# Moving and tying steps in a four-layer graph network kernel on Trainium2: normalisation, root rows, score vectors, diagonal and feature sums

## The chip, the core and the metric

The kernel runs on one core of one Trainium2 chip. The metric is device time in microseconds (us) of one execution. Work is spread over five engines, each with its own queue that it works through in order: TensorE (PE in the profile; its weight loads are PEld), VectorE (DVE), ScalarE (ACT), GpSimd (POOL) and SyncE (SP), which here only issues transfers. An engine that needs what another makes waits at that instruction, and everything behind it in its queue waits too.

## The reference

The input is `x` (2708 x 512, fp32), a sparse but densely stored adjacency `adj` (2708 x 2708) and the weights. Four layers, each followed by a residual and a layer normalisation:

```python
deg = max((adj != 0).sum(-1), 1)
# layer 0: the positive mask, divided by the root of its row count, is added to adj
head = mask / max(sqrt((mask * mask).sum(-1)), EPS)          # mask = adj > 0
inc = adj + head
x = layernorm(x + (inc @ x) / inc.sum(-1))
# layer 1: gated sum of an attention and a plain graph convolution
gate_a = sigmoid(concat(adj @ x, x) @ Wa.T + ba)              # gate_b alike with Wb, bb
h = x @ W_sa
s_left, s_right = h @ a_sa[:D], h @ a_sa[D:]
e = where(adj != 0, exp(-leaky_relu(s_left[:, None] + s_right[None, :])), 0)
x_a = (e / (e.sum(1) + 1e-5)) @ h
x_b = adj @ (x @ W_gcn) + b_gcn
x = layernorm(x + sigmoid(gate_a * x_a + gate_b * x_b))
# layer 2: three hops
p = x; out = x @ w[0]
for i in 1..3: p = adj @ p; out = out + p @ w[i]
x = layernorm(x + out)
# layer 3: degree-normalised convolution with self loops, and a skip
a_norm = rsqrt(deg)[:, None] * (adj + I) * rsqrt(deg)[None, :]
x = layernorm(x + relu((a_norm @ x + x) @ W + b))
```

## The kernel before

**Tiling.** The 2708 rows are two halves of 1354, each of 11 tiles of 128 rows (the last is partly filled). `KT` is 11, `HD` 256, `D` 512, `DC` 4. Each large product `adj @ X` in fp32 is a sweep: it works with the four quarters of the matrix (11, 12, 21, 22) and of the features (B11, B12, B21, B22) and forms seven products instead of eight, as in Strassen's scheme. For this VectorE makes sums of matrix tiles (`comb`, L403; in the later sweeps L1226) and sums of features, named T1 to T4 (`sums`, L352 to L355; L224 in the first sweeps). TensorE accumulates the products in PSUM banks (`accu`, `accc`, `accd`, `acca`), by L458 and L467 in sweeps 0 to 2 and by L1281 in sweeps 3 to 6. VectorE and ScalarE carry the results out. The letters A, B, C and D behind a name are groups of 3, 2, 3 and 2 of the ten full tiles, one SBUF buffer with room for three tiles each; the third part of a B or D buffer ("spare part") can hold other data.

**The sweeps.** Sweep 0 is layer 0, with the matrix prepared on the way: ScalarE turns raw tiles into masks (`mask`, L712 and L713), TensorE counts them (`cnt`, L724), VectorE takes the inverse root of the counts (`count_row`, L743 to L753, with one root on ScalarE, L749), TensorE spreads the roots over all partitions by transposes (`pr`, L761, in `spread_row`), ScalarE copies them out (`row`, L764), and VectorE adds mask times root to each matrix tile (`prep0`, L779 and L780). Each output tile is normalised in `done0`: statistics on VectorE (L555, L557, L559, L562), the power on POOL (`rstd`, L560), the scaling on ScalarE (L565), then the store to DRAM (`X<-o`, L149, POOL). Sweep 1 is `adj @ x` for layer 1. In it the score vectors are spread over the partitions, and each tile of x is multiplied with them (`score`, L923), which gives `s_left`, `s_right` and the gates' shares (`scores_end`, L928 and following); `score_rows` and, for the degrees, `rows` send them to DRAM as rows through `to_rows` (L937 transpose `ps_r`, L939 copy, L940 store). Sweep 2 is the attention, sweeps 3 to 5 the hops, sweep 6 layer 3, which adds the scaled diagonal to tiles of the matrix or of its saved sums (`As`) by `add_diag` (L1240).

**The score vectors before.** `start0` makes `vmat`: on each of 128 partitions, for each of four chunks of the features and each of four vectors, one value (L856, L859). `spread_v` transposes each chunk of each vector, broadcast over 128 columns, on TensorE (`pv`, L911, 16 transposes), and ScalarE copies the halves (L914, 8 copies) into eight spare parts of sweep 1's features.

**Order.** The kernel is a list of events, `at(position, function, hold)`. Positions are in units, 28 of them to a sweep (sweep s starts at 28 s; one of the seven products of a range of columns is about one unit). The list is sorted by position and run once to build the program; a tile framework then orders instructions by its own priorities and inserts the waits. `hold` ties an event's instructions behind the one before them on their engine in the list. So a shift of a position can also change the built order of other instructions.

```python
for p, _, fn in sorted(events, key=lambda e: e[:2]):
    fn()
...
    p = last if n < 3 * strict else done if n in held else {}
```

Of the kernel before, what the change touches and what calls it, by code (L numbers as in the profile page):

```python
# [68 lines left out]
def gnn_kernel(ctx: ExitStack, tc: tile.TileContext, x, adjT, w_sa, a_sa, w_gcn, b_gcn, wab, bab, w_hop, w_out,  # L69
# [48 lines left out]
    vmat = const.tile([P, DC, 4], F32, name="vmat")  # L118
# [4 lines left out]
    def feature(nm):  # L123
# [8 lines left out]
            for R0, w in RANGES for h in range(2)}  # L132
    DROW = [dram.tile([1, KT * P], F32, name=f"DR{h}", tag=f"DR{h}") for h in range(2)]
# [168 lines left out]
    def next_x2(base, src, ext_src=None, one=False, plus=False, swapped=False):  # L302
# [43 lines left out]
        def sums(g):  # L346
            i = slice(0, 2 if g in "BD" and ext_src is None else 3)
            part = lambda t: t[:, i, :]
            for s in ("T1", "T2", "T4"):
                group(s, g)  # L350
            t = {s: part(groups[s, g][0]) for s in SETS}
            nc.vector.tensor_tensor(t["T1"], t["T3"], t["B11"], ALU.subtract)  # L352
            nc.vector.tensor_tensor(t["T2"], t["B22"], t["T1"], ALU.subtract)
            nc.vector.tensor_tensor(t["T3"], t["B22"], t["T3"], ALU.subtract)
            nc.vector.tensor_tensor(t["T4"], t["B21"], t["T2"], ALU.subtract)  # L355
            for s in ("T1", "T2", "T3", "T4"):
                groups[s, g][1].update(range(3))
# [12 lines left out]
        for i, g in enumerate("ACBD"):  # L370
            at(base + 4.2 + 0.3 * i, lambda g=g: sums(g), True)


    def sweep(base, ranges, prep=None, extra=None, done=None, first=False, late=None, sums=False, save=False):
        A, spare = {}, {}
        nk = KW
        for r, (R0, n) in enumerate(ranges):
# [35 lines left out]
            if plain:  # L413
                when = {"11": (-4.0, 0.2), "12": (-3.8, 0.2), "21": (-2.4, 0.4), "22": (-1.6, 0.4)}
                pw = {"11": (-0.9, 0.6), "12": (-0.3, 0.6), "21": (3.3, 0.9), "22": (4.1, 0.9)}
# [137 lines left out]
    def layernorm(dsts, y, w, on_scalar=False):  # L553
# [9 lines left out]
        for d, c0, c1 in dsts:  # L563
            if on_scalar:
                nc.scalar.activation(d[:w], y[:w, c0:c1], AF.Identity, bias=rstd[:w, 0:1], scale=rstd[:w, 1:2])  # L565
                continue
# [228 lines left out]
    def extra0(pb, r, R0, n, A):  # L795
        if r == 0:
            for h, p, d in ((0, -3.7, 0.05), (1, 1.9, 0.055)):
# [12 lines left out]
                at(pb + p + d * 22 + 0.1 * h, lambda h=h: spread_row(R0, n, h))  # L810
        if r + 1 < len(RANGES0):
            R1, n1 = RANGES0[r + 1]
            for h, p, d in ((0, 1.0, 2.5), (1, 3.8, 2.5)) if r else ((0, 3.2, 2.2), (1, 5.4, 2.1)):
# [6 lines left out]
                at(pb + p + d + 0.15, lambda h=h: spread_row(R1, n1, h))  # L820
# [7 lines left out]
    def done0(p0, dp, last, R0, n, h, C, tiles):  # L828
        for i, (t, lo, w) in enumerate(tiles):
# [5 lines left out]
            def b(t=t, lo=lo, w=w, got=got):  # L835
# [3 lines left out]
                o = targets(t, last and not h, "o")  # L839
                layernorm(o, y, w, not last)  # L840
                store(X1[t], o, w)
# [3 lines left out]
            at(p, b)  # L845

    def start0():
# [4 lines left out]
        for n in range(2):  # L852
            v = nat("va")
            nc.scalar.dma_start(out=v, in_=bcast(a_sa[:, n * D : (n + 1) * D], D))
            for c in range(DC):
                nc.vector.scalar_tensor_tensor(y, ws[c], 1.0, v, ALU.mult, ALU.mult,  # L856
                                               accum_out=vmat[:, c, n : n + 1])
        for c in range(DC):
            nc.vector.tensor_copy(vmat[:, c, 2:4], wab_sb[:, DC + c, :])  # L859
            nc.vector.tensor_copy(wab_pad[:, c, 0:2], wab_sb[:, c, :])  # L860
# [44 lines left out]
    def spread_v():  # L905

        homes = [spare_part(s, g) for g in "BD" for s in ("B11", "B22", "T1", "T2", "T3", "B21")][:8]
        for j in range(4):
            ps = bank("pv")
            for c in range(DC):  # L910
                nc.tensor.transpose(ps[:, c * P : (c + 1) * P], vmat[:, c, j : j + 1].to_broadcast([P, P]), ident)  # L911
            for e in range(2):
                V[j, e] = homes[2 * j + e]
                nc.scalar.copy(V[j, e], ps[:, e * HD : (e + 1) * HD])  # L914

    at(S[1] + 0.85, spread_v)
# [38 lines left out]
    for R0, n in RANGES:  # L955
        for h in (1, 0):
            for k in tiles_of(R0, n):
# [3 lines left out]
                at(S[1] + 0.7 + 0.95 * i, go)  # L961
                at(S[1] + 1.1 + 0.95 * i, lambda t=h * KT + k, w=wt(k): score(t, w, got1))
                i += 1
            at(S[1] + 1.12 + 0.95 * (i - 1), lambda R0=R0, h=h, ts=tiles_of(R0, n): scores_end(R0, h, ts))
            at(S[1] + 1.6 + 0.95 * (i - 1), lambda R0=R0, h=h, ts=tiles_of(R0, n): score_rows(R0, h, ts))
    at(S[1] + 1.13 + 0.95 * (i - 1), scores_over)

    def extra1(pb, r, R0, n, A):
# [37 lines left out]
        at(pb + 3.2, lambda: rows(1))  # L1006
        at(pb + 5.2, lambda: end(0))
        at(pb + 5.8, lambda: rows(0))
# [186 lines left out]
    def sweep2(base, ext, done, on_diag=False):  # L1195
        nk = K2 + ext
        u = 2 / 7
        for g, (i0, n) in enumerate(RANGES2):
            Q, C = {}, {}
            for j, m in enumerate(ORDER2[g]):  # L1200
# [42 lines left out]
                for p, q, pos in ((0, 0, -0.52), (1, 0, -0.51), (1, 1, 0.59), (0, 1, 4.04)):  # L1243
                    for k in range(nk) if on_diag and op != "12" else ():
                        at(b + u * (pos + 0.8 * k / nk), lambda p=p, q=q, k=k, f=add_diag: f(p, q, k))
# [369 lines left out]
```

## Time and profile before

| what | value |
|---|---|
| median of 3 runs | 2874.45 us (2873.52 to 2877.68) |
| profiled execution | 2874.17 us |
| its span in the trace | 2872.1 us |
| mean granted TensorE clock | 0.998 |
| TensorE busy | 2826.4 us, 98% |
| VectorE busy | 2197.7 us, 77% |
| ScalarE busy | 546.3 us, 19% |
| GpSimd busy | 617.6 us, 22% |
| moved by DMA | 510.04 MB, mean 178 GB/s |

In a line of a group or of the timeline stand the start, the length, the engine, the line of the kernel, the instruction, the tile it writes and the tiles it reads, shapes, and the number of instructions taken together (x8); in brackets the idle time of the engine before it, and what ended it. A line of the waits reads: engine, its tile and line, what it waited for, the total in us, how often, the longest. A stretch of 361 us is one sweep.

### The profile page before, as it was taken

Reading aid. Unit: us, or ns where it says so; the run is one execution under the profiler, and the core shown is the slowest. Engines: PE = TensorE matmul, PEld = TensorE weight load, DVE = VectorE, ACT = ScalarE, POOL = GpSimd, SP = SyncE. Lnnn points to the kernel's source line nnn. Section 1 sums busy time; section 2 is a strip of 40 time slices with the busy share of each in tenths; the row PEclk is TensorE's granted clock in tenths of the full one; section 3 lists DMA queues with packets and bytes.
Section 4 is the critical chain, followed back from the end, with each engine's and each line's share of the span. In section 5 each row is a group of like instructions: output and inputs, shape, how many; then the busy total and the mean of one; then the engine's idle time right before and its main releaser. Section 6 shows DMA issues by size and latency. Waiting matters only on the chain. (4 is left out here: it accounts for less than half of the span.)

```text
span 2872.1 us, 37476 instructions
## 1 busy us (share of the span) xinstructions
PE 2826.4 (98%) x10963; PEld 1870.2 (65%) x10963; DVE 2197.7 (77%) x5670; ACT 546.3 (19%) x1119; POOL 617.6 (22%) x1113
## 2 busy tenths in 40 slices
PE   7999999999999999999999999999999999999998
PEld 5656665658765656766666666666666666666665
DVE  6989799667636554655699788887888878799987
ACT  4554200101146444641100000000000100100001
POOL 0223233223310101123213033030330211501202
PEclk9999999999999999999999999999999999999999
DMA  7666466355534333565668667566675665754542
GB/s 232 204 200 191 143 213 225 114 163 167 191 107 135 111 115 97 168 193 153 202 203 242 204 193 239 172 209 197 198 234 173 187 196 177 228 172 146 177 141 92
DMA packets 368524, 510.04 MB, mean 178 GB/s; under 512 B 63424, under 2 KB 321700, under 8 KB 368320
## 3 DMA queue, kind: packets, MB, share of 16 engines
q1 hardware_dynamic: 302392, 370.56, 43.8%
q0 software_dynamic: 49344, 126.38, 13.1%
q10 hardware_dynamic: 16584, 10.71, 1.3%
q8 instruction: 87, 1.43, 0.2%
q14 instruction: 117, 0.96, 0.1%
HBM read 423.77 MB, written 83.65 MB: 177 GB/s over the span
## 5 line engine op out<-in xcount | busy, mean ns | idle before, releaser
L1226 DVE TENSOR_TENSOR z<-z 128x339 f32<-128x339 f32 (+1 forms) x966 | 454.6, 504 | 12.6 <-PE accu L1281 3.4
L1299 ACT COPY q<-accu 128x338 f32<-128x338 f32 (+1 forms) x84 | 34.6, 443 | 1004.5 <-PE accu L1281 1002.7
L560 POOL TENSOR_TENSOR rstd<-rstd,neg_half 128x1 f32<-128x1 f32 (+3 forms) x91 | 59.3, 652 | 755.8 <-DVE rstd L559 494.9
L1281 PE MATMUL accc<-s,t 128*128 128x338 f32 (+1 forms) x644 | 198.2, 450 | 0.0
L1281 PE MATMUL accu<-z,t 128*128 128x338 f32 (+1 forms) x644 | 194.0, 448 | 1.5 <-DVE z L1226 1.5
L1281 PE MATMUL accd<-z,t 128*128 128x338 f32 (+1 forms) x644 | 193.9, 448 | 0.6 <-DVE q L1363 0.6
L1281 PE MATMUL accc<-z,t 128*128 128x338 f32 (+1 forms) x644 | 193.5, 448 | 0.5 <-ACT q L1299 0.5
L1414 POOL DMA_DIRECT2D Y<-y x192 | 105.0, 553 | 366.7 <-DVE y L1409 333.7
L403 DVE TENSOR_TENSOR a<-a,a 128x384 f32<-128x384 f32 (+2 forms) x330 | 162.6, 511 | 22.5 <-PE accu L458 21.7
L1281 PEld LDWEIGHTS accc<-s,t 128*128 128x128 f32 x644 | 120.9, 190 | 64.1 <-issue 7.5
L1281 PEld LDWEIGHTS accc<-z,t 128*128 128x128 f32 x644 | 122.0, 190 | 61.6 <-issue 1.0
L1281 PEld LDWEIGHTS accu<-z,t 128*128 128x128 f32 x644 | 121.7, 190 | 61.7 <-DVE z L1226 2.0
L1281 PEld LDWEIGHTS accd<-z,t 128*128 128x128 f32 x644 | 121.9, 190 | 60.5 <-DVE q L1363 1.5
L1226 DVE TENSOR_TENSOR s<-z 128x338 f32<-128x338 f32 (+1 forms) x322 | 149.7, 503 | 12.7 <-PE accc L1281 8.4
L1305 DVE TENSOR_TENSOR q<-q,accd 128x338 f32<-128x338 f32 (+1 forms) x112 | 56.0, 500 | 115.1 <-PE accd L1281 115.1
L1082 DVE SCALAR_TENSOR_TENSOR a<-a,e 128x384 f32<-128x384 f32 (+2 forms) x160 | 77.4, 507 | 51.0 <-ACT e L1081 46.3
L1080 ACT ACTIVATE e<-row,s_right 128x384 f32<-128x384 f32 (+5 forms) x176 | 96.5, 569 | 76.1 <-PE accc L458 20.4
L979 DVE SCALAR_TENSOR_TENSOR deg<-a,deg 128x384 f32<-128x384 f32 (+2 forms) x152 | 75.8, 505 | 13.6 <-DMA a<-in_adjT 11.9
L406 POOL DMA_DIRECT2D As<-a x120 | 64.9, 544 | 73.0 <-DVE a L403 70.2
L779 DVE SCALAR_TENSOR_TENSOR s<-a,row 128x384 f32<-128x384 f32 (+2 forms) x152 | 75.1, 507 | 6.0 <-ACT row L764 6.0
L1081 ACT ACTIVATE e<-e 128x384 f32<-128x384 f32 (+5 forms) x176 | 79.4, 477 | 1.8
L606 PE MATMUL ps_d<-w,xT 128*128 128x512 f32 (+1 forms) x176 | 79.2, 593 | 0.4 <-ACT xT L597 0.4
(683 smaller groups left out, 5840.4 us busy)
## 6 DMA issues: line engine op xcount, KB each, us to landing
z<-As SPq DMA_DIRECT2D x320, 169.5 KB
z<-As SPq DMA_DIRECT2D x320, 169.0 KB
a<-in_adjT SPq DMA_DIRECT2D x240, 192.0 KB
z<-in_adjT SPq DMA_DIRECT2D x240, 169.5 KB
z<-in_adjT SPq DMA_DIRECT2D x240, 169.0 KB
a<-in_adjT SPq DMA_DIRECT2D x120, 165.0 KB
a<-in_adjT SPq DMA_DIRECT2D x112, 128.0 KB
As<-a POOLq DMA_DIRECT2D x60, 192.0 KB, 3.9
```

What stands on the lines that cost most here:

```text
L403: nc.vector.tensor_tensor(A[r, dst, k][:, :n], A[r, a, k][:, :n], A[r, b, k][:, :n], op)
L406: nc.gpsimd.dma_start(out=SD[m][k * P : (k + 1) * P, R0 : R0 + n], in_=A[r, dst, k][:, :n])
L560: nc.gpsimd.tensor_tensor(rstd[:w, 1:2], rstd[:w, 0:1], neg_half[:w], ALU.pow)
L606: nc.tensor.matmul(o, lhs(c), r, start=c == 0 and n == 0, stop=c == DC - 1, skip_group_check=True)
L779: nc.vector.scalar_tensor_tensor(t[:w, :n], a[:w, :n], 0.0, row[R0, h][:w, :n], ALU.is_gt, ALU.mult)
L979: nc.vector.scalar_tensor_tensor(d[:w, :n], a[:w, :n], 0.0, d[:w, :n], ALU.not_equal, ALU.add)
L1080: nc.scalar.activation(e[:w, :n], row[R0, h][:w, :n], AF.Prelu, bias=s_right[:w, t : t + 1], alpha=0.01)
L1081: nc.scalar.activation(e[:w, :n], e[:w, :n], AF.Exp, scale=-1.0)
L1082: nc.vector.scalar_tensor_tensor(a[:w, :n], a[:w, :n], 0.0, e[:w, :n], ALU.not_equal, ALU.mult)
L1226: nc.vector.tensor_tensor(d[:, :n], Z[x + (k,)][:, :n], Z[y + (k,)][:, :n], op)
L1281: nc.tensor.matmul(B[home][:, :n], stat(v, k), a[:, :n], start=bool(start and k == 0), stop=k == nk - 1, skip_group_check=True)
L1414: nc.gpsimd.dma_start(out=rows[:, :, f * P : (f + 1) * P], in_=o[32 * f : 32 * (f + 1), : m * P].rearrange("p (b d) -> p b d", d=P))
```

## The change

Line numbers are those of the kernel before.

- Roots: `spread_row` of the first range is listed 0.18 instead of 0.1 units after `count_row` (half 1), and of later ranges 0.4 or 0.25 instead of 0.15.
- Normalisation: in `done0` the scaling L565 and the store leave event `b` and become events of their own 0.28 units later; the scaling is tied.
- Score vectors: `vmat` is laid out vector by vector; at position 10.3 one transpose, one copy and one transfer write it to DRAM (`VROW`, tag VR), and `spread_v` becomes eight broadcast transfers from there on SP's queue, at sweep 1's position 1.6 instead of 0.85.
- Scores: fetch, products and `scores_end` 1.2 units later, `score_rows` 1.9, degree rows 0.5.
- Feature sums: T1 and T2 stay at 4.2, T3 goes to 7.4 and T4 to 9.2, all tied.
- Diagonal: `add_diag` is tied for the first stage of the first group (`g == j == 0`).
- Preparation of quarters 21 and 22 in the first range: 0.1 units later.

```diff
@@
-    vmat = const.tile([P, DC, 4], F32, name="vmat")
+    vmat = const.tile([P, 4, DC], F32, name="vmat")
@@
+    VROW = dram.tile([4 * DC, P], F32, name="VR", tag="VR")
@@
-        def sums(g):
+        def sums(g, n):
             i = slice(0, 2 if g in "BD" and ext_src is None else 3)
             part = lambda t: t[:, i, :]
-            for s in ("T1", "T2", "T4"):
-                group(s, g)
+            if n == 0:
+                for s in ("T1", "T2", "T4"):
+                    group(s, g)
             t = {s: part(groups[s, g][0]) for s in SETS}
-            nc.vector.tensor_tensor(t["T1"], t["T3"], t["B11"], ALU.subtract)
-            nc.vector.tensor_tensor(t["T2"], t["B22"], t["T1"], ALU.subtract)
-            nc.vector.tensor_tensor(t["T3"], t["B22"], t["T3"], ALU.subtract)
-            nc.vector.tensor_tensor(t["T4"], t["B21"], t["T2"], ALU.subtract)
-            for s in ("T1", "T2", "T3", "T4"):
-                groups[s, g][1].update(range(3))
+            if n == 0:
+                nc.vector.tensor_tensor(t["T1"], t["T3"], t["B11"], ALU.subtract)
+                nc.vector.tensor_tensor(t["T2"], t["B22"], t["T1"], ALU.subtract)
+                for s in ("T1", "T2", "T3", "T4"):
+                    groups[s, g][1].update(range(3))
+            elif n == 1:
+                nc.vector.tensor_tensor(t["T3"], t["B22"], t["T3"], ALU.subtract)
+            else:
+                nc.vector.tensor_tensor(t["T4"], t["B21"], t["T2"], ALU.subtract)
@@
-            at(base + 4.2 + 0.3 * i, lambda g=g: sums(g), True)
+            for n, p in enumerate((4.2, 7.4, 9.2)):
+                at(base + p + 0.3 * i, lambda g=g, n=n: sums(g, n), True)
@@
-                pw = {"11": (-0.9, 0.6), "12": (-0.3, 0.6), "21": (3.3, 0.9), "22": (4.1, 0.9)}
+                pw = {"11": (-0.9, 0.6), "12": (-0.3, 0.6), "21": (3.4, 0.9), "22": (4.2, 0.9)}
@@
-    def layernorm(dsts, y, w, on_scalar=False):
+    def layernorm(dsts, y, w, on_scalar=False, late=None):
@@
-                nc.scalar.activation(d[:w], y[:w, c0:c1], AF.Identity, bias=rstd[:w, 0:1], scale=rstd[:w, 1:2])
+                fn = lambda d=d, c0=c0, c1=c1: nc.scalar.activation(d[:w], y[:w, c0:c1], AF.Identity,
+                                                                    bias=rstd[:w, 0:1], scale=rstd[:w, 1:2])
+                fn() if late is None else late.append(fn)
                 continue
@@
-                at(pb + p + d * 22 + 0.1 * h, lambda h=h: spread_row(R0, n, h))
+                at(pb + p + d * 22 + 0.18 * h, lambda h=h: spread_row(R0, n, h))
@@
-                at(pb + p + d + 0.15, lambda h=h: spread_row(R1, n1, h))
+                at(pb + p + d + (0.25 if h else 0.4), lambda h=h: spread_row(R1, n1, h))
@@
-                o = targets(t, last and not h, "o")
-                layernorm(o, y, w, not last)
-                store(X1[t], o, w)
+                got["o"] = o = targets(t, last and not h, "o")
+                layernorm(o, y, w, not last, None if last else got.setdefault("late", []))
+                if last:
+                    store(X1[t], o, w)
+
+            def c(t=t, w=w, got=got):
+                for fn in got["late"]:
+                    fn()
@@
+            if not last:
+                at(p + 0.28, c, True)
+                at(p + 0.28, lambda t=t, w=w, got=got: store(X1[t], got["o"], w))
@@
-                                               accum_out=vmat[:, c, n : n + 1])
+                                               accum_out=vmat[:, n, c : c + 1])
         for c in range(DC):
-            nc.vector.tensor_copy(vmat[:, c, 2:4], wab_sb[:, DC + c, :])
+            nc.vector.tensor_copy(vmat[:, 2:4, c], wab_sb[:, DC + c, :])
@@
         for j in range(4):
-            ps = bank("pv")
-            for c in range(DC):
-                nc.tensor.transpose(ps[:, c * P : (c + 1) * P], vmat[:, c, j : j + 1].to_broadcast([P, P]), ident)
+            src = VROW[j * DC : (j + 1) * DC, :]
             for e in range(2):
                 V[j, e] = homes[2 * j + e]
-                nc.scalar.copy(V[j, e], ps[:, e * HD : (e + 1) * HD])
-
-    at(S[1] + 0.85, spread_v)
+                nc.sync.dma_start(out=V[j, e], in_=bass.AP(tensor=src.tensor, offset=src.offset + e * HD, ap=[[0, P], [1, HD]]))
+
+    at(10.3, lambda: to_rows(vmat.rearrange("p j c -> p (j c)"), 4 * DC, VROW))
+    at(S[1] + 1.6, spread_v)
@@
-                at(S[1] + 0.7 + 0.95 * i, go)
-                at(S[1] + 1.1 + 0.95 * i, lambda t=h * KT + k, w=wt(k): score(t, w, got1))
+                at(S[1] + 1.9 + 0.95 * i, go)
+                at(S[1] + 2.3 + 0.95 * i, lambda t=h * KT + k, w=wt(k): score(t, w, got1))
                 i += 1
-            at(S[1] + 1.12 + 0.95 * (i - 1), lambda R0=R0, h=h, ts=tiles_of(R0, n): scores_end(R0, h, ts))
-            at(S[1] + 1.6 + 0.95 * (i - 1), lambda R0=R0, h=h, ts=tiles_of(R0, n): score_rows(R0, h, ts))
-    at(S[1] + 1.13 + 0.95 * (i - 1), scores_over)
+            at(S[1] + 2.32 + 0.95 * (i - 1), lambda R0=R0, h=h, ts=tiles_of(R0, n): scores_end(R0, h, ts))
+            at(S[1] + 3.5 + 0.95 * (i - 1), lambda R0=R0, h=h, ts=tiles_of(R0, n): score_rows(R0, h, ts))
+    at(S[1] + 2.33 + 0.95 * (i - 1), scores_over)
@@
-        at(pb + 3.2, lambda: rows(1))
+        at(pb + 3.7, lambda: rows(1))
         at(pb + 5.2, lambda: end(0))
-        at(pb + 5.8, lambda: rows(0))
+        at(pb + 6.3, lambda: rows(0))
@@
-                        at(b + u * (pos + 0.8 * k / nk), lambda p=p, q=q, k=k, f=add_diag: f(p, q, k))
+                        at(b + u * (pos + 0.8 * k / nk), lambda p=p, q=q, k=k, f=add_diag: f(p, q, k), g == j == 0)
```

## Prediction

> **What bounds the kernel now.** I read the busy shares first, then the waits of TensorE, then its timeline around each wait.
>
> ```profile
> PE 2826.4 (98%) x10963; PEld 1870.2 (65%) x10963; DVE 2197.7 (77%) x5670; ACT 546.3 (19%) x1119; POOL 617.6 (22%) x1113
> ```
>
> TensorE is busy 2826.4 of 2872.1 us: 45.7 us idle is all there is to win beside its own work. No big product is removed or added, so a change can win only waits, transposes, or time at a lower clock. The list of waits of TensorE (total us, times, longest) says where:
>
> ```profile
> PE cnt L724 <- DVE mask L710: 11.6, 13, 4.4
> PE pr L761 <- DVE r L753: 5.7, 4, 2.0
> PE cnt L724 <- ACT mask L713: 3.6, 2, 2.6
> PE accd L1281 <- DVE z L1226: 2.5, 6, 1.0
> PE ps_n L1388 <- DVE q L1305: 1.8, 1, 1.8
> PE accd L458 <- DVE a L403: 1.8, 3, 1.2
> PE ps_r L937 <- DVE s_left L929: 1.6, 1, 1.6
> PE ps_r L937 <- DVE y L652: 1.6, 1, 1.6
> ```
>
> The first row is the start of the program, which the change leaves alone. The rest are short waits, most of them beside a line that the diff moves. TensorE's timeline (start, length, instruction, wait before it) shows two of them six microseconds apart in sweep 0:
>
> ```profile
> 84.11 0.38 PE L724 MATMUL cnt<-ones_bf,mask 128*128 128x1 bf16 x9 [2.64 <-ACT mask L713]
> ...
> 90.96 0.54 PE L761 MATMUL pr<-ident,r 128*128 128x128 f32 x3 [1.95 <-DVE r L753]
> ```
>
> ScalarE's timeline says why the mask was late: it stood in the queue behind a normalisation that waited for its scale.
>
> ```profile
> 81.31 0.81 ACT L565 ACTIVATE o<-ld,rstd 128x512 f32<-128x512 f32 x1 [2.12 <-DVE rstd L562]
> ```
>
> Each wait is followed by a stretch at half clock (stretch; length; PE, weight loads, DVE, ACT, POOL busy; granted clock; DMA share; GB/s):
>
> ```profile
> 84.00:86.00 2.00, 1.89 (x17) 1.42 (x17) 1.93 (x6) 1.94 (x6) 0.00 (x0) 0.68 0.89 294
> 86.00:88.00 2.00, 2.00 (x9) 1.64 (x7) 1.86 (x6) 1.94 (x5) 0.00 (x0) 0.50 0.95 301
> 88.00:90.00 2.00, 1.01 (x5) 0.54 (x3) 1.77 (x7) 0.96 (x3) 0.00 (x0) 0.96 1.05 349
> 90.00:92.00 2.00, 1.04 (x13) 1.03 (x14) 1.69 (x7) 1.94 (x6) 0.00 (x0) 0.89 1.02 353
> 92.00:94.00 2.00, 2.00 (x6) 1.55 (x6) 1.86 (x5) 1.94 (x6) 0.00 (x0) 0.50 0.41 126
> ```
>
> Below, a stall is the excess of the step from one matmul's start to the next over the usual one (0.284 us a pass at 338 columns, 0.323 at 384), so it is a little longer than the listed wait.
>
> **Norm and roots in sweep 0 (72 to 370 us).** The normalisation L565 goes 0.28 units later and, in the built order, behind the masks of the next two tiles; the root transposes (L761, first group) go 15 TensorE instructions later, to the place of 95.91 us. That can free 2.80 us at 84.11, 2.11 at 90.96, and 3.4 from the two half-clock stretches (3.4 us each, so 1.7 lost in each): 8.3 us at most. *The Trainium skill* ("TensorE: Matmul & The Clock Gate", part 1, the HAM clock gate) puts the half clock behind an idle window of about 3.4 us; by it waits of 2.64 and 1.95 us cost nothing beyond themselves, and the ceiling would be 4.9. The granted clock of 0.50 decides: 8.3. But it does not all last. VectorE has hardly a gap from 81 to 194 us, so its deadlines stay: its sums L403 are ready 2.88 us before TensorE wants them at 154.53 and 2.53 before at 156.05. In the built order two products of T4A (0.65 us each) and two count groups (0.23 each) come ahead there and relieve the second. So 2.9 survives, and 5.4 is turned into waiting near 155. With each L565 its store X<-o leaves POOL 0.28 units later (3.6 us, at 361 us for a sweep of 28 units), and sweep 1's loads of T3A, queued there at 351.72, follow about 5 us later; T3A is next read at 426.0 (L224), and that hides them.
>
> At 172.75 the roots wait again (stall 0.99); they go eight matmuls (5.2 us) later, so that goes: 0.99. At 328 they go two matmuls (1.3 us) later where VectorE waited 3.41 us for their row, so its chain starts later; the POOL wait of 1.29 us for rstd at 357.23 should shrink to about 0.46, since L560 leaves POOL before the stores of T3A. The stall at 363 to 369 (2.25, T1C and T2A waiting for L403) grows by about 0.4. Sum: 2.9 + 1.0 - 0.4 = 3.5 us won.
>
> **Score vectors.** Sixteen transposes and eight ScalarE copies go; one 16x128 transpose, one copy and one POOL store come early (place 10.3), and eight SP loads. The tile pv gives the price:
>
> ```profile
> L911 PE MATMUL pv<-ident,vmat x16: 272/272/273, 437.0 to 438.7; 128*128 128x128 f32 x16
> ```
>
> They are pipelined: the next product starts 1.74 us after the first. The new transpose, by the 0.11 us step of L937, costs 0.11: 1.63 won. Its data (L856) are ready 3 us before its place. The copies were off the path. The loads are no TensorE work; their waits are the danger, below.
>
> **Scores later.** The products move 1.2 units (about 15 us) and the row transposes 1.9. Stalls at 477.44 (1.75, for s_left) and 581.77 (1.74, for y L652) go, since the transposes then stand well behind their data: 3.49. VectorE has 2.7 to 4.6 us less ahead of it at 688 and 724, where 0.32 and 0.95 were lost: 1.27. A closer deadline at 463 (1.13 us) gets 3.0 us less work ahead. The last score row ends near 751 before; its rows are fetched for sweep 2 about 813, so 25 us later still leaves 37. S1 in all: 1.63 + 3.49 + 1.27 = 6.4 us.
>
> **Diagonal.** In S6 VectorE stood still twice:
>
> ```profile
> 2456.10 0.35 DVE L1240 SCALAR_TENSOR_TENSOR z<-ident,diag,z 128x128 f32<-128x128 f32 x1 [2.82 <-DMA z<-As]
> ...
> 2463.23 0.27 DVE L1240 SCALAR_TENSOR_TENSOR z<-ident,diag,z 128x46 f32<-128x46 f32 x1 [5.12 <-DMA z<-As]
> ```
>
> The tie puts this addition behind z and q work that has its data. Behind it stood the z sums, and TensorE paid 0.38 + 1.12 at 2463 to 2469 and 2.00 at 2476.81 (ps_n for q): 3.5 won. The 7.9 us of VectorE time returned also cover the next near deadlines (0.4 to 1.8 us at 2491 to 2513). Bounds: 0, if the additions still head the queue, to 3.5.
>
> **Feature sums.** Sixteen additions a sweep (in S6 eight of 0.95 us and eight of 0.68) stood together from place 4.2. The T3 additions go to 7.4 and T4's to 9.2; in S6 that takes 6.5 us of VectorE work from the crowded place. Stalls behind them at 1443, 1805 and 2166 were 0.42 each (1.27), in S6 1.64 at 2528 and 0.70 at 2535 (2.34): 3.6 won. VectorE has 3.7 to 7.4 us in hand where the T3 sums land (2557 to 2570) and at least 4.3 where T4's land (2575 to 2590), against 3.3 us each. If that cover were gone, up to 6.5 us in S6 would come back. The other places (degree rows, the two preparations, 0.1 unit) issue the same work at places without a near wait: 0.
>
> **The sum.** 3.5 + 6.4 + 3.5 + 3.6 = 17.0 us. The profiled execution before took 2874.17 us (span 2872.1 and 2.1 around it), 0.3 under the median 2874.45. 2874.4 - 17.0 = 2857.4. I take off none for loads being late, as likeliest.
>
> **The danger: SP's queue.** The eight vector loads must wait until TensorE has read the tile whose spare third they fill, and in the built order they stand in the midst of sweep 0's loads. The skill ("DMA: Bandwidth & Descriptors", anatomy of one DMA) says that such a wait is made by the issuing sequencer before dispatch; the row agrees, and against the change it says that everything behind waits too:
>
> ```profile
> 336.69 7.03 SPq L394 DMA_DIRECT2D a<-in_adjT  x3
> 343.81 0.44 SPq L149 DMA_DIRECT2D ld<-in_x  x1
> 346.62 6.82 SPq L394 DMA_DIRECT2D a<-in_adjT  x4
> ```
>
> The first vector load would be reached at 329.9 and released at 341.0 (last read of B11B); the second at 334.1 and 347.0 (B11D); four more hold 1.7, 1.7, 4.8 and 3.7. Behind the second stand the r rows and three 165 KB loads issued at 336.7, 339.5 and 343.4 before; VectorE reads them from 351.3 on, in the new order about 2.9 us later. Issued from 347.0 and after 2.6 us of r rows, the first leaves at 349.7; such a load issued at 332.45 had its packets done by 334.3. Landed at 351.6 against 354.2: about 2 us to spare. By the freely issued row the cost is 0, by the rule with packets crowded it is up to 4. I take 0, with 4 in the range.
>
> **Rivals.**
> *SP's queue decides: slower.* The holds sum to 11.1 + 12.9 + 1.7 + 1.7 + 4.8 + 3.7 = 36 us. If more than 17 of these (47%) reach VectorE and TensorE, nothing is left of the gain; if all do, 2874.4 - 17 + 36 = 2893. Against it: the margin just worked out.
> *No change in net.* TensorE's gains meet VectorE's deadlines in sweep 0 and S1 (3.5 + 4.8 back), and the T3 and T4 sums cost in S6 what the diagonal gives: 17.0 - 8.3 - 6.5 = 2, time 2872.
> *The larger gain.* VectorE's chain from 81 to 155 is itself quicker, since masks and counts come earlier: the other 5.4 survives, time 2852.
> *Half of the gain.* SP's loads late by 4, the diagonal not freed (3.5): 17.0 - 7.5 = 9.5, time 2865.
>
> **How the numbers follow.** A measurement of this kernel can tell about 0.2%, 5.7 us. Chances: the sum as worked out 0.46, half of it 0.22, the larger gain 0.16, no net change 0.09, slower 0.07. The first three, 0.84, are faster; 2872 is "same". The range 2850 to 2869 takes in those three with their unknown costs and leaves out the last two, 0.16; the likeliest alone is 2854 to 2861.
>
> **What would show it.** Right: no wait of L724 for L713 near 84, clock near 1.0 from 84 to 96, perhaps a wait of L458 for L403 near 155; no wait of L937 for L929 or L652; no stop of VectorE at L1240 near 2463; no wait of L1281 for L1226 at 2528. Wrong: VectorE waiting for DMA a<-in_adjT between 345 and 360; TensorE waiting near 2560 to 2600; a clock of 0.5 at a new place.

## The result, and the profile after

The changed kernel takes 2862.6 us (median of 5 runs, 2862.36 to 2865.06); beside it the kernel before took 2874.53 us (5 runs, 2873.52 to 2877.68). The ratio is 0.9958, 95% interval 0.9946 to 0.997: faster by 0.42%, 12 us, where 17 were forecast. The time lies inside the range of 2850 to 2869, 5 us above the predicted one and above the 2854 to 2861 given as the likeliest case alone. The profiled execution took 2862.54 us, span 2860.8, mean granted clock 0.998 as before. Most lines moved by 6 to 15 in the listing: L724 is now L732, L713 L721, L761 L769, L753 L761, L565 L571, L458 L464, L403 L409, L562 L568, L560 L566, L1281 L1296, L1226 L1241.

Busy shares, changed kernel:

```profile
PE 2821.3 (99%) x10948; PEld 1868.6 (65%) x10948; DVE 2196.7 (77%) x5670; ACT 542.2 (19%) x1112; POOL 616.8 (22%) x1114
```

TensorE has 15 instructions less (16 transposes out, one in), and the other engines do about the same work. TensorE's waits (total, times, longest):

```profile
PE cnt L732 <- DVE mask L718: 11.5, 12, 4.7
PE pr L769 <- DVE r L761: 5.8, 3, 2.6
PE accd L464 <- DVE a L409: 3.8, 4, 1.9
PE cnt L732 <- ACT mask L721: 2.9, 4, 1.0
PE accd L1296 <- DVE q L1378: 1.8, 1, 1.8
```

The waits for `s_left`, for y, for `z` and for `ps_n` of before (1.6, 1.6, 2.5, 1.8) are gone from the head of the list. The second row, 5.7 before, has not shrunk, with a longest wait of 2.6 instead of 2.0. The third has doubled, from 1.8 to 3.8. The fifth is new. TensorE's timeline of the changed kernel shows where:

```profile
85.64 0.38 PE L732 MATMUL cnt<-ones_bf,mask 128*128 128x1 bf16 x9 [0.84 <-ACT mask L721]
...
91.35 0.54 PE L769 MATMUL pr<-ident,r 128*128 128x128 f32 x3 [2.63 <-DVE r L761]
...
154.26 0.91 PE L464 MATMUL accd<-a,T1C 128*128 128x384 f32 x2 [1.35 <-DVE a L409]
...
366.03 4.18 PE L464 MATMUL accd<-a,T1C 128*128 128x330 f32 x8 [1.92 <-DVE a L409]
...
2590.53 1.41 PE L1296 MATMUL accd<-z,t 128*128 128x338 f32 x4 [1.78 <-DVE q L1378]
```

The mask's 2.64 at 84 became 0.84, but the roots wait 2.63 where they waited 1.95. At 366 and at 2590 TensorE loses more than before, and after 366 the clock is at half (columns as in the prediction: stretch, length, PE, weight loads, DVE, ACT, POOL, clock, DMA share, GB/s):

```profile
366.00:368.00 2.00, 1.97 (x4) 1.22 (x5) 2.00 (x6) 0.00 (x0) 0.00 (x0) 0.61 0.68 208
368.00:370.00 2.00, 2.00 (x5) 1.30 (x4) 2.00 (x6) 0.00 (x0) 0.00 (x0) 0.54 0.55 103
```

The kernel before has full clock there.

To divide the 11.3 us by place I took the start of the same TensorE instruction in both traces. The table gives how much later (+) or earlier (-) than in the kernel before each stretch ends than it began, in us. Places are times in the kernel before; S1 and S6 are sweeps 1 and 6.

| kernel | 67 to 193 | 345 to 397 | S1, 397 to 740 | S6, 2450 to 2543 | 2543 to end |
|---|---|---|---|---|---|
| predicted | -3.9 | +0.4 | -6.4 | -5.8 | 0 |
| changed kernel | -0.7 | +2.3 | -7.1 | -6.8 | +1.8 |
| e1_v_tied | +1.9 | +1.7 | -6.6 | -6.8 | +1.8 |
| e2_v_pe | -0.3 | +1.3 | -4.7 | -6.8 | +1.8 |
| e3_roots_last | +2.2 | +0.2 | -7.1 | -6.8 | +1.8 |
| e4_norm_undone | -2.6 | +2.3 | -6.8 | -6.8 | +3.8 |
| e10_roots_undone | +1.7 | -0.7 | -7.2 | -6.8 | +3.5 |
| e11_norm_roots_undone | +1.1 | +3.9 | -7.3 | -6.8 | +1.8 |
| e5_t4_early | -0.8 | +2.1 | -7.5 | -6.8 | +1.6 |
| e6_t4_late | +1.9 | +1.5 | -7.1 | -6.8 | +9.0 |
| e7_diag_untied | +1.9 | +1.8 | -7.1 | -3.1 | +3.5 |
| e8_v_and_scores_undone | +2.1 | +1.3 | +0.2 | -6.8 | +3.8 |
| e9_sums_undone | -0.7 | +2.0 | -6.8 | -6.0 | +0.1 |
| e12_best | -2.7 | -0.6 | -7.1 | -6.0 | +0.1 |

Sweeps 3 to 5 gave 0.5 in the changed kernel, where 1.3 were forecast. These are single profiled executions. S1 and S6 up to 2543 repeat to some tenths. The other columns repeat less well: the changed kernel, e5, e6, e7 and e9 have the same program up to S1, and from 345 to 397 they lose 1.5 to 2.3; the first and the last column can differ by 2 to 3 us for the same instructions, as shown at the end.

### The profile page after: what moved, and what is told of

It reads as the page before. It is cut to its first block, busy times and chain, and to the rows that moved or that the text cites. A ratio compares the mean times of both kernels' runs of the same rounds, so it can differ in the third digit from the quotient of the medians.

```text
span 2860.8 us, 37431 instructions
## 1 busy us (share of the span) xinstructions
PE 2821.3 (99%) x10948; PEld 1868.6 (65%) x10948; DVE 2196.7 (77%) x5670; ACT 542.2 (19%) x1112; POOL 616.8 (22%) x1114
## 4 chain that ended last, share of the span: by engine, by line
PE 88%; DVE 6%; issue 2%; DMA 2%; SPq 1%; POOL 1%; ACT 1%; POOLq 0%; DVEq 0%; ACTq 0%
PE accu L1296 12%; PE accd L1296 12%; PE accc L1296 12%; PE accd L464 9%; PE accu L464 8%; PE accc L464 8%; PE ps_d L614 6%; PE acca L1296 6%; PE acca L464 4%; PE accr L1367 2%; PE ps L653 2%; PE accr L1371 1%; DVE z L1241 1%; DVE z L662 1%; DVE s L787 1%
## 5 line engine op out<-in xcount | busy, mean ns | idle before, releaser
L1241 DVE TENSOR_TENSOR z<-z 128x339 f32<-128x339 f32 (+1 forms) x966 | 454.6, 501 | 11.5 <-PE accu L1296 3.2
L566 POOL TENSOR_TENSOR rstd<-rstd,neg_half 128x1 f32<-128x1 f32 (+3 forms) x91 | 60.5, 665 | 754.6 <-DVE rstd L565 509.1
L1296 PE MATMUL accc<-s,t 128*128 128x338 f32 (+1 forms) x644 | 198.2, 450 | 0.0
L1296 PE MATMUL accd<-z,t 128*128 128x338 f32 (+1 forms) x644 | 193.9, 448 | 1.8 <-DVE q L1378 1.8
L1296 PE MATMUL accc<-z,t 128*128 128x338 f32 (+1 forms) x644 | 193.5, 448 | 0.5 <-ACT q L1314 0.5
L1296 PE MATMUL accu<-z,t 128*128 128x338 f32 (+1 forms) x644 | 193.8, 448 | 0.0
L409 DVE TENSOR_TENSOR a<-a,a 128x384 f32<-128x384 f32 (+2 forms) x330 | 161.8, 509 | 23.7 <-PE accu L464 22.7
L1296 PEld LDWEIGHTS accc<-s,t 128*128 128x128 f32 x644 | 120.9, 190 | 64.0 <-issue 7.5
L1296 PEld LDWEIGHTS accc<-z,t 128*128 128x128 f32 x644 | 122.0, 190 | 61.5 <-issue 1.0
L1296 PEld LDWEIGHTS accd<-z,t 128*128 128x128 f32 x644 | 121.9, 190 | 61.6 <-DVE q L1378 2.5
L1296 PEld LDWEIGHTS accu<-z,t 128*128 128x128 f32 x644 | 121.9, 190 | 59.8 <-issue 0.5
L1241 DVE TENSOR_TENSOR s<-z 128x338 f32<-128x338 f32 (+1 forms) x322 | 149.9, 502 | 10.9 <-PE accc L1296 8.4
```

Source lines behind the costliest of these rows:

```text
L409: nc.vector.tensor_tensor(A[r, dst, k][:, :n], A[r, a, k][:, :n], A[r, b, k][:, :n], op)
L1241: nc.vector.tensor_tensor(d[:, :n], Z[x + (k,)][:, :n], Z[y + (k,)][:, :n], op)
L1296: nc.tensor.matmul(B[home][:, :n], stat(v, k), a[:, :n], start=bool(start and k == 0), stop=k == nk - 1, skip_group_check=True)
```

## The experiments

Each edit is made on the changed kernel, and each kernel computes the whole reference. Times are medians, with the kernel before on the same chip beside them. Of e5 to e9 there is one run each, so their times prove little and they are used for their places. The intervals of the ratios all overlap that of the changed kernel, so what an edit is worth is read by place from the traces, and the medians only stand beside it.

**Where do the vector loads stand?** Only the order in SP's queue is changed: the eight loads are tied where the list puts them.

```diff
-    at(S[1] + 1.6, spread_v)
+    at(S[1] + 1.6, spread_v, True)
```

> Changed kernel, but the eight vector loads are tied to their place in the list, so that they stand behind sweep 0's matrix loads on SP. Theory Q (SP's queue): the waits of VectorE for DMA a<-in_adjT near 354.5 and 355.3 (0.80 and 0.33 us) go, the wait of TensorE before T1C near 366 falls from 1.92 to about 0.8, and the half clock from 366 to 370 (1.7 us lost) goes: 2859.8 to 2861.5. Theory R (roots): the later root row alone makes T1C late; the wait stays near 1.9 and the time at 2862.6.

Measured: 2864.5 us (5 runs, 2860.49 to 2865.42; before 2873.79, 15 runs), ratio 0.9964, 0.995 to 0.9978. In the changed kernel SP's timeline held the loads as predicted (340 and 346), and VectorE did wait for a late tile (VectorE's timeline, changed kernel):

```profile
354.51 0.50 DVE L787 SCALAR_TENSOR_TENSOR s<-a,row 128x330 f32<-128x330 f32 x1 [0.80 <-DMA a<-in_adjT]
```

Those waits (0.80, and 0.33 at 355.33) are gone with the tie, but TensorE is only 0.6 us better off from 345 to 397, which is within the 1.5 to 2.3 that the same program gave: a wait of 1.60 for `rstd` takes their place on VectorE at 352, and the half clock after the stall stays (368.4 to 371.8). So the loads' place is not enough to explain the stall at 366.

**The vectors' transposes put back.**

```diff
-            src = VROW[j * DC : (j + 1) * DC, :]
+            ps = bank("pv")
+            for c in range(DC):
+                nc.tensor.transpose(ps[:, c * P : (c + 1) * P], vmat[:, j, c : c + 1].to_broadcast([P, P]), ident)
...
-    at(10.3, lambda: to_rows(vmat.rearrange("p j c -> p (j c)"), 4 * DC, VROW))
-    at(S[1] + 1.6, spread_v)
+    at(S[1] + 0.85, spread_v)
```

> Changed kernel, but the score vectors are spread by 16 transposes and 8 copies again, at 0.85 units, with the scores left late. By the step of the prediction this costs 1.63 us of TensorE in sweep 1. Theory Q: SP's queue is freed as well, so sweep 0 wins 1.1 to 2.8: 2861.4 to 2863.1 in all. Theory R: sweep 0 stays: 2864.2.

Measured: 2867.26 us (11 runs, 2865.59 to 2870.34), ratio 0.9978, 0.9969 to 0.9986. In S1 it wins 4.7 instead of 7.1: the transfers are worth 2.4 there, where the price of the transposes gave 1.63. TensorE loses 1.7 at the transposes, and the rest mostly at 687, where it waits 0.78 for y instead of 0.18. By medians e2 is 4.7 us behind the changed kernel; its profile is of the fastest of the 11 runs, so 2.4 is what one execution shows. From 345 to 397, without any such load in the queue, 1.3 is still lost, with the same wait of 1.92 for T1C: something else is late there.

**Only the last range's roots early again** (position 0.15, as before).

```diff
-                at(pb + p + d + (0.25 if h else 0.4), lambda h=h: spread_row(R1, n1, h))
+                at(pb + p + d + (0.15 if r == 2 else 0.25 if h else 0.4), lambda h=h: spread_row(R1, n1, h))
```

> Changed kernel, but the roots of the last range of sweep 0 are transposed at 0.15 units as before. Theory R: VectorE's chain from 329 starts 1.3 us earlier, the wait before T1C falls to 0.6 and the half clock goes: 2859.5 to 2861.3. Theory Q: the chain starts earlier but then waits longer for DMA a<-in_adjT (1.1 becomes about 2.4), T1C stays late: 2862.6.

Measured: 2863.01 us (4 runs, 2859.45 to 2863.93), ratio 0.996, 0.9945 to 0.9975. From 345 to 397 it loses 0.2 instead of 2.3, with the vector loads where the changed kernel has them, and the waits for DMA are gone. With the late normalisation, the later roots at 328 are thus what made VectorE late at 366. The whole run is no faster than the changed kernel: its sweep 0 up to 193 stood 2.9 us worse with the same program up to there.

**The late normalisation ("norm") undone**, with the roots left late.

```diff
-                layernorm(o, y, w, not last, None if last else got.setdefault("late", []))
-                if last:
-                    store(X1[t], o, w)
+                layernorm(o, y, w, not last, None)
+                store(X1[t], o, w)
...
-            if not last:
-                at(p + 0.28, c, True)
-                at(p + 0.28, lambda t=t, w=w, got=got: store(X1[t], got["o"], w))
```

> Changed kernel, but the normalisation L565 and its store are back in their old place, with the roots left late. The prediction gave the masks' move 2.8 us at 84 and a half-clock stretch: if masks are what counts, the wait of L724 for L713 near 84 comes back with its half clock and sweep 0 loses 1.4 to 3, 2864 to 2866. Rival: VectorE's queue sets the root transposes at 91 and the sums at 154 in any case, so that the waits only change place: 2862 to 2863.

Measured: 2862.68 us (4 runs, 2861.54 to 2862.99), ratio 0.996, 0.9945 to 0.9975: no different. TensorE's stall for the mask is back (2.80 at 83.59), but the roots do not wait at all, since what stands ahead of them now comes later. Stalls from 64 to 193, worked out as in the prediction: before 2.80 + 2.11 + 0.99 = 5.9; changed kernel 0.65 + 1.00 + 2.79 + 0.76 + 1.51 = 6.7; here 2.80 + 0.76 + 1.18 = 4.7. The norm's move wins nothing beside the later roots; it moves the wait from the mask to the roots.

**The roots undone, with the norm late.**

```diff
-                at(pb + p + d * 22 + 0.18 * h, lambda h=h: spread_row(R0, n, h))
+                at(pb + p + d * 22 + 0.1 * h, lambda h=h: spread_row(R0, n, h))
...
-                at(pb + p + d + (0.25 if h else 0.4), lambda h=h: spread_row(R1, n1, h))
+                at(pb + p + d + 0.15, lambda h=h: spread_row(R1, n1, h))
```

> Changed kernel, but all root transposes are at their old places, the normalisations late. If the later roots are what costs (T1C near 366, 2 us, and the reordered sums near 98): sweep 0 ends 2 to 4 us earlier, 2859 to 2861. If the late normalisation is what costs, sweep 0 stays or gets worse: 2862 to 2865.

Measured: 2865.51 us (5 runs, 2864.99 to 2867.03; before 2874.81, 10 runs), ratio 0.9966, 0.9953 to 0.9979. The roots wait 6.55 us at 92.46 (a stall of 6.71), and from 67 to 193 it is 2.4 us worse than the changed kernel, 1.7 of them half clock. From 345 to 397 nothing is lost: it gains 0.7, with the vector loads still held in SP's queue. So neither case of the expectation holds alone: the later roots cost at 366 and win at 92.

**Norm and roots both undone**: the edits of the last two together.

```diff
-                at(pb + p + d * 22 + 0.18 * h, lambda h=h: spread_row(R0, n, h))
+                at(pb + p + d * 22 + 0.1 * h, lambda h=h: spread_row(R0, n, h))
...
-            if not last:
-                at(p + 0.28, c, True)
```

> Changed kernel with both the late normalisation and the later roots undone, so that of sweep 0 only the vector loads in SP's queue are left of the change. The prediction gave the two 3.5 us: by it 2866 us. By the traces so far the two together cost about 0 to 2 us: 2860.5 to 2862.6, the stalls of 2.80, 2.11 and 0.99 back near 84, 91 and 172, and T1C near 366 late by the loads alone.

Measured: 2866.44 us (6 runs, 2864.71 to 2868.05; before 2874.81), ratio 0.997, 0.9957 to 0.9982. This is the run in which the danger in SP's queue shows. Its sweep 0 has the old norm and roots and differs from before by the store and the loads of the score vectors and a preparation 0.1 units later, and it loses 3.9 us from 345 to 397. SP's timeline:

```profile
327.29 4.53 SPq L400 DMA_DIRECT2D a<-in_adjT  x2
342.64 0.33 SPq L924 DMA_DIRECT2D B11B<-VR  x1
343.07 0.56 SPq L150 DMA_DIRECT2D ld<-in_x  x1
...
348.72 7.08 SPq L400 DMA_DIRECT2D a<-in_adjT  x2
355.90 0.38 SPq L924 DMA_DIRECT2D B11D<-VR  x1
```

SP issued nothing from 331.8 to 342.6 and then a crowd of loads. POOL's timeline of the same kernel shows who paid:

```profile
346.81 0.59 POOL L150 DMA_DIRECT2D X<-o  x1 [1.39 <-ACT o L571]
...
353.19 0.54 POOL L150 DMA_DIRECT2D B11B<-X  x1 [4.73 <-DMA X<-o]
353.74 0.56 POOL L566 TENSOR_TENSOR rstd<-rstd,neg_half 128x1 f32<-128x1 f32 x1
```

The reload of the features waits in POOL's queue for the store of X. From the start of the store to that of the reload, 6.4 us pass; in the kernel before, 2.6:

```profile
345.18 0.59 POOL L149 DMA_DIRECT2D X<-o  x1 [1.39 <-ACT o L565]
...
347.81 0.54 POOL L149 DMA_DIRECT2D B11B<-X  x1 [0.98 <-DMA X<-o]
```

Behind the reload stands the next tile's power L566, and VectorE waits for it 3.38 us at 354.34 (2.27 more at 362.76). So late loads reached VectorE not through the matrix tiles that the prediction watched, but through a store of X that landed late, and through POOL's queue behind it. In e4, which has the early norm too, the same is seen with 5.0 us from store to reload and a wait of 3.69 us for L566 at 355.43. With the late norm the store can be as late and cost nothing there, since the next power has left POOL before the reload (POOL's timeline, changed kernel):

```profile
349.37 0.59 POOL L150 DMA_DIRECT2D X<-o  x1 [1.40 <-ACT o L571]
351.35 0.68 POOL L566 TENSOR_TENSOR rstd<-rstd,neg_half 128x1 f32<-128x1 f32 x1 [1.39 <-DVE rstd L565]
...
355.95 0.54 POOL L150 DMA_DIRECT2D B11B<-X  x1 [3.37 <-DMA X<-o]
```

That the crowd of loads is what slowed the store is read from these rows. The last kernel below comes nearest to isolating it: it has the early norm and the same last roots, with the loads tied out of the way, and it gains 0.6 where e11 loses 3.9; but its earlier ranges have the later roots, so it is not a change of one thing.

**The scores early again, with the vectors of e2** and the degree rows at their old places.

```diff
-                at(S[1] + 1.9 + 0.95 * i, go)
-                at(S[1] + 2.3 + 0.95 * i, lambda t=h * KT + k, w=wt(k): score(t, w, got1))
+                at(S[1] + 0.7 + 0.95 * i, go)
+                at(S[1] + 1.1 + 0.95 * i, lambda t=h * KT + k, w=wt(k): score(t, w, got1))
...
-            at(S[1] + 3.5 + 0.95 * (i - 1), lambda R0=R0, h=h, ts=tiles_of(R0, n): score_rows(R0, h, ts))
+            at(S[1] + 1.6 + 0.95 * (i - 1), lambda R0=R0, h=h, ts=tiles_of(R0, n): score_rows(R0, h, ts))
```

> Changed kernel, but the score vectors are spread by transposes at 0.85 units and the score products, rows and degree rows are at their old places. Against the run with the transposes alone undone, sweep 1 loses the stalls that the prediction names, 1.75 at 477, 1.74 at 581, 0.32 at 688 and 0.95 at 724: 4.8 us. Rival: the stalls at 477 and 581 come from VectorE being late out of sweep 0 and not from the scores' place: 2 us or less.

Measured: 2875.02 us, one run (before 2876.13). TensorE's timeline has both stalls back:

```profile
481.67 0.27 PE L952 MATMUL ps_r<-ident,s_left 128*3 128x128 f32 x1 [1.72 <-DVE s_left L944]
...
585.99 0.27 PE L952 MATMUL ps_r<-ident,s_left 128*3 128x128 f32 x1 [1.57 <-DVE y L659]
```

A third of 1.25 stands at 694; e2, with the scores late, has 0.94 of it. Between 397 and 740 it falls 7.3 us behind the changed kernel, e2 2.4: the scores are worth 4.9, against the 3.49 + 1.27 = 4.8 of the prediction.

**The diagonal untied.**

```diff
-                        at(b + u * (pos + 0.8 * k / nk), lambda p=p, q=q, k=k, f=add_diag: f(p, q, k), g == j == 0)
+                        at(b + u * (pos + 0.8 * k / nk), lambda p=p, q=q, k=k, f=add_diag: f(p, q, k))
```

> Changed kernel, but the diagonal additions L1255 are untied again. The prediction gave the tie 3.5 us: VectorE stops at L1255 for DMA z<-As again (2.8 and 5.1 us) and TensorE loses 3.5 us from 2450 to 2480. Of it up to 1.8 comes back at 2590, where TensorE waits for VectorE in any case: 1.7 to 3.5 us slower than the changed kernel at the end. Rival: the feature sums' move frees VectorE and hides the diagonal: no loss.

Measured: 2871.51 us, one run (before 2876.13). TensorE's timeline has the two waits back:

```profile
2465.11 0.84 PE L1296 MATMUL accd<-z,B21D 128*128 128x339 f32 x2 [0.95 <-DVE z L1241]
...
2473.47 0.63 PE L1403 MATMUL ps_n<-ident,q 128*128 128x128 f32 x4 [1.84 <-DVE q L1320]
```

By 2543 it stands 3.7 us worse than the changed kernel (-3.1 against -6.8), so the tie is worth its 3.5. The wait at 2590 does not change. The run as a whole is 8.9 us behind the changed kernel; 2.6 of that arise between 67 and 193, with the same program, and 1.7 come from a half-clock stretch after the wait at 2590 that the changed kernel's profile does not have.

**The feature sums all at 4.2 again.**

```diff
-            for n, p in enumerate((4.2, 7.4, 9.2)):
+            for n, p in enumerate((4.2, 4.21, 4.22)):
```

> Changed kernel, but the T3 and T4 additions stand beside T1 and T2 at 4.2 again. The prediction gave their move 1.27 us (0.42 before accd at 1443, 1805 and 2166) and 2.34 us in sweep 6 (1.64 and 0.70): these stalls come back. If the move itself caused the new wait at 2590, that falls from 1.94 to about 0.8 as before: 3.6 us slower up to 2570, 2.4 at the end. Rival: with the diagonal tied, VectorE has room enough for all sums at 4.2: no stall comes back, 0.

Measured: 2863.84 us, one run (before 2874.81). The three stalls of 0.43 are back near 1439, 1802 and 2163. In S6 the 1.64 and the 0.70 at 2528 and 2535 are not: it gains 6.0 by 2543 against 6.8, and then keeps it, since the stall at 2590 is 0.76 as before, not 1.94. TensorE's timeline:

```profile
2591.17 1.40 PE L1296 MATMUL accd<-z,t 128*128 128x338 f32 x4 [0.60 <-DVE q L1378]
```

The sums' move wins 0.8 in S6 and gives 1.7 back at 2590, in these two profiles.

**T4 of the sums elsewhere**: to 7.6 in one kernel, to 10.4 in S6 in the other.

```diff
-            for n, p in enumerate((4.2, 7.4, 9.2)):
+            for n, p in enumerate((4.2, 7.4, 7.6)):
```

```diff
-            for n, p in enumerate((4.2, 7.4, 9.2)):
+            for n, p in enumerate((4.2, 7.4, 10.4 if base == S[6] else 9.2)):
```

> Changed kernel, but the T4 additions stand at 7.6 instead of 9.2, right behind T3's. In sweep 6 VectorE then has them before 2561, where it stood idle 1.42 us. Theory V (VectorE is full from 2563 to 2592 and sets TensorE's wait of 1.94 before accd at 2590.5): at most the idle 1.4 us is used, so that the two waits of 0.49 and 1.94 sum to 1.0 or more. Rival: the T4 additions alone cause the wait, and it goes wholly: 1.8 less, no wait near 2590.

> Changed kernel, but in sweep 6 the T4 additions stand at 10.4 instead of 9.2. Theory V: VectorE has up to 3.3 us less ahead of the sum that TensorE waits for at 2590.5, so that wait falls from 1.94 to near 0; the additions then meet the waits of L653 at 2603 and 2615 (0.97 and 0.71), which grow by as much or less: 0 to 1.8 us won at 2640. Rival: the wait at 2590 is not VectorE's load but the late products (accr) it needs: it stays at 1.9.

Measured: 2861.46 us early and 2872.53 us late, one run each (before 2876.13). Early, the stalls at 2588 to 2590 are 0.49 + 1.51 instead of 0.49 + 1.94. Late, where up to 1.8 us were expected to be won, the wait for `q` stays 1.78 and a new one comes at 2619 (TensorE's timeline):

```profile
2592.96 2.25 PE L1296 MATMUL accd<-z,t 128*128 128x338 f32 x4 [1.78 <-DVE q L1378]
...
2619.76 5.24 PE L1296 MATMUL accc<-z,t 128*128 128x338 f32 x10 [4.73 <-ACT q L1314]
```

From 2543 to the end the late one loses 9.0 us where the changed kernel loses 1.8, in the new wait and in half-clock stretches at 2593 and 2617 to 2624. Neither place of T4 removes the wait at 2590; only all sums at 4.2 bring it down to 0.6.

**Four placements together**: norm as before, only the last roots early, vector loads tied, sums at 4.2 in S6 alone. (The expectation says "late" of the last range's roots; the edit makes them early.)

```diff
-            for n, p in enumerate((4.2, 7.4, 9.2)):
+            for n, p in enumerate((4.2, 4.21, 4.22) if base == S[6] else (4.2, 7.4, 9.2)):
...
-                at(pb + p + d + (0.25 if h else 0.4), lambda h=h: spread_row(R1, n1, h))
+                at(pb + p + d + (0.15 if r == 2 else 0.25 if h else 0.4), lambda h=h: spread_row(R1, n1, h))
...
-            if not last:
-                at(p + 0.28, c, True)
-                at(p + 0.28, lambda t=t, w=w, got=got: store(X1[t], got["o"], w))
...
-    at(S[1] + 1.6, spread_v)
+    at(S[1] + 1.6, spread_v, True)
```

> Four placements together: the range norm of sweep 0 as in the kernel before, only the last range's roots late, the score vectors' loads tied in the order of SyncE's queue alone, and the feature sums as before in the last stage only. Everything else as in the changed kernel. Theory (the parts add up as the single runs showed them): sweep 0 stands 0.5 to 3 us ahead of the kernel before at 193 us and within 1 us of it at 397, S1 gives 7, S3 to S5 0.5 to 1, S6 5 to 6, so 2858 to 2861.5 us and a span some 12 to 15 us under that of before. Rival (half-clock stretches after the remaining waits take the gain of sweep 0 back, and the single parts don't add up): 2862 to 2865 us, no different from the changed kernel.

Measured: 2858.45 us (5 runs, 2857.43 to 2859.2; before 2874.84, 9 runs), ratio 0.9941, 0.9928 to 0.9955, span 2856.7. Its slowest run is 3 us under the changed kernel's fastest; the two were timed at different times, each beside the kernel before, and the intervals of the ratios overlap. From 345 to 397 it gains, as only e10 does beside it. SP's queue goes from 328 to 354 in the order of the kernel before, and POOL's timeline is quick again:

```profile
343.41 0.59 POOL L150 DMA_DIRECT2D X<-o  x1 [1.39 <-ACT o L571]
...
346.10 0.54 POOL L150 DMA_DIRECT2D B11B<-X  x1 [1.04 <-DMA X<-o]
```

## Why the prediction was right, and where not

The time fell into the range, but the account held only in part: scores, diagonal and transfers won what was said or more, sweep 0 did not, and all three things named as signs of being wrong appeared: VectorE waiting for `a<-in_adjT` at 354, TensorE waiting at 2590, and half clock at a new place, 366.

**Score vectors, 1.63.** Right: 1.7 at the transposes by e2; the transfers' 2.4 in S1 holds about 0.6 more at 687, which was not in the sum.

**Scores later, 4.76.** Right: 4.9 by e8 against e2 in one profile each, with both named stalls at their places. The 1.27 put at 688 and 724 is not shown apart.

**Diagonal, 3.5.** Right: 3.7 by e7, with the two waits that the prediction named.

**Feature sums, 1.27 and 2.34.** The first is about right: the three stalls come and go with the move. The failed term is 2.34 in S6. I counted the stalls at 2528 and 2535 as the sums' own, but e9 keeps the sums together at 4.2, with the diagonal tied, and they are gone all the same: the VectorE time that the tie returned (7.9 us, which I credited to near deadlines up to 2513 only) had most likely covered them; a kernel with the tie alone was not run. And "at least 4.3 where T4's land (2575 to 2590)" did not hold: 1.7 came back at 2590, at a place that I had named as a sign against me. Net, the move costs S6 0.9 us (-5.9 without it against -5.0), and 1.7 more in executions where half clock follows the wait.

**Norm and roots in sweep 0, 3.5.** This is the step that failed most. I had "2.9 survives" with the loss near 155. Nothing survived: the stalls from 82 to 92 alone are 5.20 us where they were 4.91, and 1.51 at 154 comes on top. What the profile gained up to 193 (0.7) is half clock, 1.7 us of it instead of 3.4, and other executions of the same program lost 5.1. The roots' transposes were moved behind the mask's wait, but their data were not made earlier. VectorE's timeline of the kernel before has the root chain behind the running sums:

```profile
86.50 3.17 DVE L775 TENSOR_TENSOR run<-run,a 128x256 f32<-128x256 f32 x7
89.59 0.28 DVE L745 TENSOR_SCALAR r<-cnt 128x1 f32<-128x1 f32 x3
```

That of the changed kernel has the same, 0.4 us later:

```profile
86.89 3.17 DVE L783 TENSOR_TENSOR run<-run,a 128x256 f32<-128x256 f32 x7
89.98 0.28 DVE L753 TENSOR_SCALAR r<-cnt 128x1 f32<-128x1 f32 x3
```

So when TensorE came sooner it waited longer for r; e4 shows the same gain to be had without the norm's move. "The stall at 363 to 369 grows by about 0.4" was too small by 1.9 us; by e3 2.1 of the 2.3 (1.3 at least, by the scatter) come with the later roots at 328, part of it as the half clock from 366. (The forecast that the wait for `rstd` at 357 shrinks from 1.29 to 0.46 held: it is 0.46, at 352.) With the early norm the roots do not act so: 2.3 are lost with late ones (e4), 3.9 with early ones (e11). The parts do not add. Taken with both undone (e11) and the same vector loads, norm and roots are worth 2866.44 - 2862.6 = 3.8 us by medians, close to 3.5, but for a reason that I did not have: with the early norm (e11) 3.9 is lost at 345 to 397, with the late one and the same early roots (e10) 0.7 is gained. The sum looks right and the account is not.

**The danger, 0.** The holds are where I put them (340 and 346 against 341.0 and 347.0), and the margin of 2 us nearly covers the tiles: 1.1 us of waiting for them. But I asked only who reads the held loads. The store of X on POOL, whose landing POOL itself waits for, was not in the account; its price at 345 to 397 was up to 3.9 us (e11), by what stands beside it. In the changed kernel it is not clear of the scatter: e1 puts it at 0.6, and the same program differs by 0.8 there.

By place against the forecast: sweep 0 up to 397 +4.7 (+1.2 for -3.5), S1 -0.7, sweeps 3 to 5 +0.8, S6 +0.8. The rival "half of the gain" (2865) came nearer in time than the sum (2857.4), but one of its two reasons, a diagonal that is not freed, did not happen, and the other, late loads, came to less than its 4. That the likeliest case and this rival both lie in the range is why the number held. The loss in sweep 0 stood only in "no change in net" (3.5 back where TensorE's gains meet VectorE's deadlines), whose other terms, in S1 and S6, did not come.

## What to carry to other kernels

Credit a stall to one cause only after asking what the other parts of the change already cover: here the diagonal paid for what the sums were to win, and with early roots the late norm covered what the held loads would have cost. Where a load is held and others crowd behind it, look not only for who reads them but for every store in those microseconds whose landing another queue waits for. Moving a consumer behind a wait wins only if its own producer is not bound by the order of a third engine.

## What the hardware showed that I had not expected

The changed kernel and e6 are the same program up to S6, and in both the roots wait 2.63 us near 91.4. What follows differs. The stretches of the changed kernel (as before: stretch, length, PE, weight loads, DVE, ACT, POOL, clock, DMA share, GB/s):

```profile
92.00:94.00 2.00, 1.51 (x14) 1.29 (x15) 1.83 (x6) 1.94 (x5) 0.00 (x0) 0.84 0.68 188
94.00:96.00 2.00, 2.00 (x7) 1.17 (x7) 1.93 (x6) 1.97 (x5) 0.00 (x0) 0.50 0.71 198
96.00:98.00 2.00, 2.00 (x9) 1.30 (x10) 0.63 (x2) 1.97 (x7) 0.00 (x0) 0.80 0.57 148
98.00:100.00 2.00, 2.00 (x19) 1.70 (x18) 1.94 (x6) 2.00 (x6) 0.54 (x1) 1.00 0.32 113
```

and those of e6:

```profile
92.00:94.00 2.00, 1.76 (x14) 1.27 (x13) 1.86 (x5) 1.94 (x5) 0.00 (x0) 0.50 0.71 188
94.00:96.00 2.00, 2.00 (x7) 1.50 (x5) 1.90 (x6) 1.97 (x5) 0.00 (x0) 0.50 0.73 198
96.00:98.00 2.00, 2.00 (x7) 0.84 (x6) 0.70 (x3) 1.37 (x4) 0.00 (x0) 0.50 0.48 109
98.00:100.00 2.00, 2.00 (x6) 1.55 (x6) 0.22 (x1) 2.00 (x7) 0.05 (x1) 0.50 0.46 157
```

Summed as time at less than full clock, 64 to 152 us costs 1.7 us in the changed kernel and 5.1 in e6; of these 3.4 us more, 2.6 are left at 193. Over the profiles with the same sweep 0 the loss was 1.7 (the changed kernel, e5, e9) or 5.1 (e1, e3, e6, e7): one or three half-clock stretches of 3.4 us after the same waits. The kernel before had two (3.4) in its profile, and its 15 runs in one comparison scatter from 2869.86 to 2878.2 us. So a single profile's sweep 0 says nothing finer than about 3 us, and the early stages were judged here by their stalls and by medians. The wait at 2590 shows it more plainly. Eight profiles have the same program in S6 (the changed kernel, e1 to e4, e8, e10, e11) and the same wait of 1.78 for `q`. In five no half clock follows, in three (e4, e8, e10) one stretch does, which costs 1.7 us. These are 2592 to 2596 in the changed kernel and in e10:

```profile
2592.00:2596.00 4.00, 4.00 (x19) 3.29 (x18) 2.34 (x7) 0.00 (x0) 0.00 (x0) 1.00 0.33 91
2592.00:2596.00 4.00, 4.00 (x12) 2.99 (x11) 1.23 (x5) 0.00 (x0) 0.00 (x0) 0.58 0.34 91
```

So the length of the wait alone does not settle it; what does, no run here shows. In sweep 0, as in the kernel before, none of the waits that these stretches follow is as long as the 3.4 us of idle that the Trainium skill ("TensorE: Matmul & The Clock Gate", part 1) puts ahead of the half clock: the longest is 2.64.
